# A conv–scan–attention kernel on one core: convolution taps over 128 + 2×64 channels, column sums placed first, in-projection issued between convolution steps

## The chip, the cores and the metric

One core of one Trainium2 chip. The metric is the device time of one execution in microseconds (us). Five engines have instruction queues of their own: TensorE (PE; its weight loads are listed as PEld), VectorE (DVE), ScalarE (ACT), GpSimd (POOL) and SyncE (SP), which issues most DMAs. Each engine takes its instructions in program order and waits on semaphores of the others.

## What is computed

Input `x` is (4, 64, 64, 96). The reference, cut to what matters (per image; `bq` is the sign, `bilinear(x, W) = bq(x) @ (s * bq(W - mean(W))).T + b`):

```python
xz = bilinear(group_norm(x), W_in)            # 96 -> 2*192; only signs of x - mean matter
xp, z = split(xz)
t  = bq(xp + move0_b)                         # signs, 192 channels
t  = conv3x3(t, sc * sign(conv_W))            # 192 -> 192 channels, 9 taps
t  = prelu(t + conv_b + rp_b0) + rp_b1 + xp
u  = silu(t)
for k in 4 directions:                        # rows, columns, and both reversed
    dt, B, C = bilinear(u in direction k, Wl[k])
    delta = softplus(bilinear(dt, Wd[k]) + dt_bias)
    h = exp(delta * A) * h + delta * u * B    # scan over 4096 positions, 192 x 16 states
    y += sum(h * C) + D * u
x = x + bilinear(layernorm(y) * silu(z), W_out)
x = x + linear attention(layernorm(x)) ; x = x + quantized FFN(layernorm(x))
```

## The kernel before

`hybrid_kernel` sets up tiles and calls `run`. The work on each of the NB = 4 images has three parts: a **prologue** (everything up to the scan's operands), the **scans** and an **epilogue** (layer norm, out-projection, attention, FFN).

`Scans.run` is the main loop: 1536 pieces of 128 (32 channels × 4 states) × 1024 positions. A piece is a decay (`dA`, ACT exponential), an injection (`w`, POOL product), a scan (DVE), a product with C (on DVE or POOL, chosen when the program is built by a running tally of both), and a reduction over states (PE, line 1340). The prologue of image b + 1 and the epilogues are generators; one step of them is issued per piece (`next(back)`), so their instructions stand between those of the scans. The prologue of image 0 has nothing to hide behind and runs first, beside the generator `weights()`; `interleave` takes one step of each in turn. In the code this case is `alone = True`; below it is called the head.

The order on every engine is the order of the program text; nothing is rescheduled. What sets it around the change:

- `weights()` issues all loads of weights at its start, on SP: `w_in`, then twelve loads of the convolution's weights (`cw_t`, by input channel, for the products; `cw_n`, by output channel, for their mean size), then the small ones (among them `wrow`, `meanw`, whose rows are gathered in 4-byte elements), ending with `bff`. On ACT it issues `pvd`, twelve loads of `sbR` and 24 loads of `anm` (the A matrix, 32 × 16 elements of 4 bytes each); the signs `wis` of `w_in` come behind these on ACT. Then it signs and transposes the weights (PE, with copies on DVE and POOL) in some 25 steps.
- `prologue`: column sums of x (`csum`, line 514), the negative mean `negm`, eight transposes `xps` whose signs go to `xsT` and whose values go to DRAM through `xb` tiles; the **in-projection**, 16 steps (h, q) for two halves of 96 channels and eight blocks of 512 positions, each with two products (`ix`, `iz`) and two ACT signs: `tp` (the padded image that the convolution reads, in two tiles of 96 channels) and `sz` (the sign of z, stored to DRAM). Then the **convolution**: 16 parts (h, q), each with 18 products of 96×96 weights (9 taps × 2 input halves, line 616) into one PSUM half, then `cz` (line 658), `v` (DVE) and `r` (ACT). In the next part, between the products: two `scalar_tensor_tensor` on DVE, `sg` (signs, copied by three DMAs into `xg`), the exponentials `e`, and `u` on DVE, stored to DRAM in rows (`ud`) and, after a copy on POOL, in columns (`utd`).
- then, for directions (1, 3) and afterwards (0, 2): `xr`, `acc` (the product with Wl), `bcd` and `sgd` to DRAM; `g` is read back, transposed on PE (`gp`, line 761), written to DRAM as `gTd`, and `load_signs` (lines 1161, 1162) reads it into one of two tiles `gT`, from which `prepare` makes delta (line 1202 and on).
- DMAs that go out later are put on a list (`Later`) and issued on SP some steps on. SP is one queue: a DMA is issued after all that stand before it.
- temporary tiles `f32(...)` (xb, sz, v, r, sg, e, u) turn through a pool of 8; the pool `h` has 2.

Of the kernel before, what the change touches and what calls it, by code (L numbers as in the profile page):

```python
# [11 lines left out]
F32 = mybir.dt.float32  # L12
# [13 lines left out]
CH = 1024  # L26
# [19 lines left out]
def halves(src):  # L46

    yield slice(0, 96), 0, src[0:96, 0]
    yield slice(0, 32), 1, src[96:128, 0]
    yield slice(32, 96), 1, src[0:64, 1]  # L50
# [3 lines left out]
def hybrid_kernel(ctx: ExitStack, tc: tile.TileContext, a: dict, out: bass.AP):  # L54
# [14 lines left out]
    def ctile(name, shape, dt=F32):  # L69
        return const.tile(shape, dt, name=name, tag=name)  # L70
# [54 lines left out]
    woutT = ctile("woutT", [96, 2, DM], BF16)  # L125
    cw = ctile("cw", [96, 2, 9, DN], F8)
    csc = ctile("csc", [96, 2])
# [4 lines left out]
    gTs = [ctile(f"gT{i}", [128, 4, 128], F8) for i in range(2)]  # L132
    sbias, cbias = ctile("sbias", [96, 2]), ctile("cbias", [96, 2])

# [23 lines left out]
    def weights():  # L158
# [28 lines left out]
        def transposed(dst, srcs):  # L187

            count[0] += 1
            ps = p.ps.tile([128, 1024], BF16, name=f"tps{count[0]}", tag=f"y{count[0] % 2}")  # L190
            at = 0
            for src in srcs:
                n, f = src.shape
                nc.tensor.transpose(ps[:f, at : at + n], src, identb[:n, :n])
                at += n
            nc.vector.tensor_copy(dst, ps[:f, 0:at], saturate=False if dst.dtype == F8 else None)

        wi = temp("wi", [128, 3, DM], F32)
        nc.sync.dma_start(wi, a["w_in"].rearrange("(t p) j -> p t j", p=128))

        cuts = (slice(0, 5 * DN), slice(5 * DN, 9 * DN))
        cwf, cwn = ([[temp(f"{nm}{h}{i}", [96, s.stop - s.start]) for i, s in enumerate(cuts)] for h in range(2)] for nm in ("cwf", "cwn"))
        for ts, src in ((cwf, a["cw_t"].rearrange("p h t d -> p h (t d)")), (cwn, a["cw_n"])):
            for rows, h, s in halves(src):
                for i, cut in enumerate(cuts):
                    nc.sync.dma_start(ts[h][i][rows], s[:, cut])
        wl = [temp(f"wl{o}", [128, DN], F32) for o in range(2)]
# [31 lines left out]
        nc.gpsimd.memset(bff, 0.0)  # L239
        nc.sync.dma_start(bff[DM : DM + 1, :], a["bff"])  # L240
        nc.scalar.dma_start(pvd, a["pv"][:, :, SD : SD + 3 * NK])
        nc.gpsimd.memset(sbR, 0.0)
# [5 lines left out]
        for g in range(NG):  # L248
            src = a["al"][32 * (g % 4) : 32 * (g % 4) + 32, g // 4].rearrange("d k (q j) -> j d (k q)", j=4)
            for j in range(4):  # L250
                nc.scalar.dma_start(anm[j::4, g, :], src[j])
        for t in gTs + [wdz]:
            nc.gpsimd.memset(t.bitcast(F32), 0.0)

        nc.vector.tensor_tensor(sbias, pv[:, :, B_X], pv[:, :, MOVE0], ALU.add)
        wim = negmean("wim", wi, DM)
        wis = temp("wis", [128, 3, DM], BF16)
        for t in range(3):
            nc.scalar.activation(wis[:, t, :], wi[:, t, :], AF.Sign, bias=wim[:, t : t + 1])
        transposed(winT, [wis[:, t, :] for t in range(3)])  # L260
        yield
        part = temp("part", [96, 2, 2])
        for h in range(2):
            for i, cut in enumerate(cuts):
                nc.scalar.activation(
                    cw[:, h].rearrange("p t d -> p (t d)")[:, cut], cwf[h][i], AF.Sign, saturate=False
                )
                nc.vector.tensor_reduce(part[:, h, i : i + 1], cwn[h][i], AX.X, ALU.add, apply_absolute_value=True)
# [66 lines left out]
        nc.vector.tensor_reduce(dsum, pv[:, :, DSK : DSK + NK], AX.X, ALU.add)  # L335
        nc.scalar.activation(anm, anm, AF.Exp)
        nc.vector.tensor_scalar(anm, anm, -1.0, None, ALU.mult)
        nc.vector.tensor_reduce(sum4, ident.rearrange("p (d j) -> p d j", j=4), AX.X, ALU.add)
# [94 lines left out]
def run(c):  # L433

    made, first = c.weights(), prologue(c, 0, c.xts)
    lanes = [made, first]
    while (0, 1) not in c.ready:
        interleave(lanes)
        c.later.tick()
# [40 lines left out]
def prologue(c, b, xts=None):  # L480
# [11 lines left out]
    with tc.tile_pool(name=f"xg_{b}", bufs=1) as xgp:  # L492
# [3 lines left out]
        with tc.tile_pool(name=f"cv_{b}", bufs=1) as cvp:  # L496
            xsT = cvp.tile([DM, L], F8, name=f"xsT_{b}", tag="xsT")
            tflat = [cvp.tile([96, (IH + 2) * (IW + 2)], F8, name=f"tp{h}_{b}", tag=f"tp{h}") for h in range(2)]
            tpad = [t.rearrange("p (h w) -> p h w", w=IW + 2) for t in tflat]
# [55 lines left out]
            for h in range(2):  # L555
                nc.gpsimd.memset(tflat[h].bitcast(F32), 0.0)
            for h in range(2):
                for q in range(NQ8):
                    cols = slice(512 * q, 512 * q + 512)
                    px, pz = bank(f"ix{h}{q}", 0)[0:96], bank(f"iz{h}{q}", 1)[0:96]  # L560
                    for ps, c0 in ((px, 96 * h), (pz, DN + 96 * h)):
                        nc.tensor.matmul(ps, c.winT[:, c0 : c0 + 96], xsT[:, cols], start=True, stop=True)
                    yield
                    nc.scalar.activation(
                        tpad[h][:, 1 + 8 * q : 9 + 8 * q, 1 : 1 + IW], px.rearrange("p (h w) -> p h w", w=IW),
                        AF.Sign, scale=pv[:, h, S_X : S_X + 1], bias=c.sbias[:, h : h + 1], saturate=False,
                    )
                    sz = f32(f"sz{h}{q}").bitcast(BF16)[0:96, 0:512]
                    nc.scalar.activation(
                        sz, pz, AF.Sign, scale=pv[:, h, S_Z : S_Z + 1], bias=pv[:, h, B_Z : B_Z + 1]  # L570
                    )
                    c.later.store(c.szd[b][h][:, cols], sz)


            yield
            parts = [(h, q) for h in range(2) for q in range(NQ8)]
            taps = [(j, t) for j in range(2) for t in range(9)]
            one = lambda h: slice(h, h + 1)
            prev = turned = None
            two = c.p.dA.tile([128, CH], F32, name=f"cv2_{b}", tag="dA") if alone else None  # L580
            utp = sub.enter_context(tc.tile_pool(name=f"ut_{b}", bufs=1))
# [23 lines left out]
            for n, part in enumerate(parts + [None]):  # L605
                if part:
                    h, q = part
                    nm = f"{h}{q}"
                    at = 512 * (n % 2)
                    ps = (two[:, at : at + 512] if alone else bank("cv" + nm, 0))[0:96]  # L610
                for s in range(4 if alone else 5):
                    if part:
                        per = 5 if alone else 4
                        for j, t in taps[per * s : min(18, per * s + per)]:
                            dy, dx = divmod(t, 3)
                            nc.tensor.matmul(  # L616
                                ps, c.cw[:, j, t, 96 * h : 96 * h + 96],
                                tpad[j][:, 8 * q + dy : 8 * q + dy + 8, dx : dx + IW],
                                start=(j == 0 and t == 0), stop=(j == 1 and t == 8),
                            )  # L620
                    if s == 0 and turned:
                        by_columns(*turned)
                        turned = None
# [46 lines left out]
        with tc.tile_pool(name=f"rw_{b}", bufs=1) as rw:  # L670
# [4 lines left out]
            tbg, sgg = (t.rearrange("p (g r) -> p g r", r=64) for t in (tbc, sgn))  # L675
            g2 = rw.tile([128, 2, 320], F8, name=f"g_{b}", tag="g")
            gw = g2.bitcast(F32)
            for o in (1, 0):
# [74 lines left out]
                if o:  # L753
                    nc.gpsimd.memset(gw[:, :, 48:80], 0.0)
                for x, k in enumerate((o, o + 2)):
                    nc.sync.dma_start(gw[:, x, 0:48], c.sgd[b][k].rearrange("(p f) -> p f", p=128))
                    yield
                    yield
                    gp = bank(f"gp{k}", k // 2).rearrange("p (s f) -> p s f", s=4)
                    for s in range(4):  # L760
                        nc.tensor.matmul(
                            gp[:, s, :], g2[:, x, 48 * s : 48 * s + 128], c.ident8, start=True, stop=True
                        )
                    yield
                    t = rw.tile([48, 4, 32], F32, name=f"gt_{b}_{k}", tag="gt", bufs=2)
                    nc.scalar.activation(t.bitcast(F8), gp[0:48], AF.Copy, saturate=False)
                    nc.sync.dma_start(c.gTd[b][k], t)
# [360 lines left out]
class Scans:  # L1128
# [6 lines left out]
    def __init__(self, c):  # L1135
# [9 lines left out]
        self.late, self.cys = None, {}  # L1145
        self.us, self.gs, self.at, self.loaded, self.sums = {}, {}, -1, set(), {}

# [213 lines left out]
    def run(self, back):  # L1361
# [4 lines left out]
        for x in range(3):  # L1366
# [5 lines left out]
            )  # L1372
        interleave(lanes)
        for q in range(NQ):
            self.load_bc(0, self.bt, 0, 0, 0, q)
            self.load_bc(1, self.ct, 0, 0, 0, q)
# [124 lines left out]
```

## Time and profile before

| | us |
|---|---|
| device time, four runs | 5529.95 to 5538.66, median 5532.41 |
| the profiled execution: device time | 5531.33 |
| the profiled execution: span, first to last instruction | 5529.5 |
| first convolution product in the head | 85.09 |
| last `r` of the convolution in the head starts | 186.45 |
| first `xr` copy | 200.69 |
| first product of `prepare` (line 1202) | 234.78 |
| first scan | 271.19 |

Busy over the span: DVE 91%, POOL 90%, ACT 65%, PE 63%. "Busy" of PE is modelled from pipelined instructions. In the timeline a row has the start, the duration, the engine, the line, the operation, output <- input and how many instructions were merged; in brackets stands the idle time of the engine ahead of it and what ended it. `SPq` and `ACTq` rows are issues of DMAs; their duration is that of the issue, not of the transfer. The windows view gives the busy time of each engine in a stretch, the granted TensorE clock (PEclk, 1.00 is full) and the DMA share.

### The profile page before, as it was taken

To read this page: it belongs to the slowest core of one execution; us is meant where nothing else is said; L and a number is where in the kernel's file an instruction comes from. 1 tells how busy PE (TensorE), PEld (TensorE's weight loads), DVE (VectorE), ACT (ScalarE), POOL (GpSimd) and SP (SyncE) were. 2 spreads that over 40 slices of the span, in tenths; PEclk is the share of its full clock that TensorE was granted. 3 is DMA by queue.
4 is the path that set the end of the run, shared out by engine and by line. 5 is a ranking of instruction groups with operands and counts; after the bars stand their busy time and mean duration, and the time that the engine had idled before them with its cause. 6 is when DMAs were issued, how large, how long until landed. Compare 5 with 4: busy or idle time off the path is not lost. (4 is left out here: it accounts for less than half of the span.)

```text
span 5529.5 us, 62184 instructions
## 1 busy us (share of the span) xinstructions
PE 3489.3 (63%) x20133; PEld 1373.0 (25%) x20133; DVE 5024.9 (91%) x3198; ACT 3568.6 (65%) x5568; POOL 4974.8 (90%) x2255
## 2 busy tenths in 40 slices
PE   5456765467656776657765686664677664445677
PEld 2222222123222222222222232221232221111223
DVE  3299999999999999999999999999999999999984
ACT  4467766677666667777666666776556775555554
POOL 2199999899999999999999999999999999999981
PEclk8666776677766776677776777666787676565787
DMA  4455765766666666676765666667666556666652
GB/s 80 120 187 192 211 199 190 237 223 207 204 192 203 195 201 211 193 239 211 221 191 185 204 205 195 199 207 230 201 214 192 181 191 202 210 201 191 207 157 60
DMA packets 613243, 1069.92 MB, mean 193 GB/s; under 512 B 225083, under 2 KB 343924, under 8 KB 611124
## 3 DMA queue, kind: packets, MB, share of 16 engines
q1 hardware_dynamic: 599428, 1065.88, 61.9%
q8 instruction: 158, 2.59, 0.2%
q10 hardware_dynamic: 13488, 0.07, 0.1%
q14 instruction: 169, 1.38, 0.1%
HBM read 833.20 MB, written 229.38 MB: 192 GB/s over the span
## 5 line engine op out<-in xcount | busy, mean ns | idle before, releaser
L404 POOL TENSOR_TENSOR w<-dl,bc 128x1024 f32<-128x1024 f32 x1536 | 3578.4, 2355 | 159.5 <-PE yp L1340 61.3
L1267 ACT ACTIVATE dA<-dl,anm 128x1024 f32<-128x1024 f32 x1536 | 1714.6, 1116 | 494.2 <-DVE w L404 279.9
L404 DVE TENSOR_TENSOR_SCAN dA<-dA,cy,w 128x1024 f32<-128x1024 f32 x711 | 1665.8, 2343 | 98.7 <-ACT dA L1267 93.6
L1340 PE MATMUL yp<-w,sum 128*32 128x256 f32 x12288 | 1287.7, 514 | 396.1 <-POOL w L404 250.0
L404 POOL TENSOR_TENSOR w<-h,bc 128x1024 f32<-128x1024 f32 x587 | 1380.7, 2352 | 115.8 <-DVE h L404 108.1
L404 DVE TENSOR_TENSOR w<-dA,bc 128x1024 f32<-128x1024 f32 x949 | 1162.3, 1225 | 48.6 <-issue 0.9
L404 DVE TENSOR_TENSOR_SCAN h<-dA,cy,w 128x1024 f32<-128x1024 f32 x441 | 1031.6, 2340 | 10.1 <-ACT dA L1267 10.0
L1340 PEld LDWEIGHTS yp<-w,sum 128*32 128x32 f32 x12288 | 315.2, 129 | 1480.3 <-issue 698.6
L1309 ACT COPY cy<-dA 128x1 f32<-128x1 f32 x715 | 112.2, 157 | 746.0 <-DVE w L404 744.2
L404 DVE TENSOR_TENSOR_SCAN dA<-dA,w 128x1024 f32<-128x1024 f32 x238 | 543.3, 2283 | 29.4 <-ACT dA L1267 20.5
L616 PE MATMUL cv<-tp,cw 96*96 96x512 fp8e5 x1152 | 371.9, 459 | 44.3 <-ACT r L656 40.3
L404 DVE TENSOR_TENSOR_SCAN h<-dA,w 128x1024 f32<-128x1024 f32 x146 | 332.5, 2278 | 10.7 <-ACT dA L1267 9.0
L1202 PE MATMUL dps<-gT,wdz 128*128 128x64 fp8e5 x1000 | 113.6, 313 | 336.3 <-ACT ys L1354 308.0
L1215 PE MATMUL dps<-sp,ident 128*128 128x512 f32 x376 | 282.2, 841 | 50.0 <-ACT dps L1211 49.9
L1345 PE MATMUL yp<-ya,back 128*128 128x256 f32 x576 | 240.4, 539 | 1.8 <-DMA ya<-y 1.0
L616 PEld LDWEIGHTS <-cw 96*96 96x96 fp8e5 x1152 | 156.2, 147 | 238.1 <-issue 188.5
L1202 PEld LDWEIGHTS <-wdz 128*128 128x128 fp8e5 x1024 | 94.8, 152 | 422.9 <-issue 389.5
L1202 PE MATMUL dps<-gT,wdy 128*128 128x64 fp8e5 x504 | 59.9, 323 | 204.1 <-ACT ys L1354 202.0
L1309 ACT COPY cy<-h 128x1 f32<-128x1 f32 x437 | 81.4, 186 | 148.1 <-DVE h L404 146.9
L1207 ACT ACTIVATE pd<-dps,dbias,pvd 128x512 f32<-128x512 f32 x188 | 143.2, 762 | 21.9 <-PE dps L1202 21.6
L1345 PEld LDWEIGHTS yp<-ya,back 128*128 128x128 f32 x576 | 124.5, 250 | 131.1 <-issue 88.6
L878 PE MATMUL yc<-eys,mean 96*96 96x512 f32 x240 | 136.3, 722 | 29.6 <-DVE vks L404 13.7
(290 smaller groups left out, 4223.3 us busy)
## 6 DMA issues: line engine op xcount, KB each, us to landing
dl<-dld SPq DMA_DIRECT2D x768, 512.0 KB
bc<-bcd SPq DMA_DIRECT2D x512, 512.0 KB
dld<-pd SPq DMA_DIRECT2D x125, 512.0 KB
yd<-ys SPq DMA_DIRECT2D x768, 64.0 KB
dld<-pd SPq DMA_DIRECT2D x126, 256.0 KB
ya<-yd SPq DMA_DIRECT2D x192, 128.0 KB
pu<-ud SPq DMA_DIRECT2D x32, 512.0 KB
pu<-utd SPq DMA_DIRECT2D x30, 512.0 KB
```

What stands on the lines that cost most here:

```text
L404: return getattr(self.eng, name)(out, *args, **kw)
L616: nc.tensor.matmul(ps, c.cw[:, j, t, 96 * h : 96 * h + 96], tpad[j][:, 8 * q + dy : 8 * q + dy + 8, dx : dx + IW], start=(j == 0 and t == ...
L878: self.c.nc.tensor.matmul(ps, w, x, start=(i == 0), stop=(i == len(pairs) - 1))
L1202: nc.tensor.matmul(pv[:, s], wd[:, k, s], gT[:, :, c0 : c0 + 16], start=(s == 0), stop=(s == 7))
L1207: nc.scalar.activation(d[:, 0], ps, AF.Abs, scale=sc, bias=bi)
L1215: nc.tensor.matmul(ps, c.ident, t, start=False, stop=True, skip_group_check=True)
L1267: c.nc.scalar.activation(t, self.dlt[i // NQ][0], AF.Exp, scale=c.anm[:, g, NQ * KORD[e] + q : NQ * KORD[e] + q + 1])
L1309: self.c.nc.scalar.copy(self.carries[g, q], h[:, CH - 1 : CH])
L1340: c.nc.tensor.matmul(y[32 * x : 32 * x + 32, g % 2, :], c.sum4, prod[:, 256 * x : 256 * x + 256], start=(q == 0), stop=(q == NQ - 1 and no ...
L1345: c.nc.tensor.matmul(y[:, g % 2, :], w, src, start=False, stop=(n == len(more) - 1))
```

## The change

Parts that go together:

1. The convolution's input channels lie as one tile of 128 channels and one tile that holds the other 64 channels twice, in its lower and its upper 64 partitions, the upper copy moved by one column. One product over the second tile so serves two taps of a line; 9 + 3 × 2 = 15 products a part. The weights lie to match in `cwA` and `cwB` (a quarter of `cwB` is zero). For the second tile the in-projection has weights `winB` (the 64 columns twice) and two ACT signs instead of one. This holds for all four images. Steps per part stay 5 (4 in the head).
2. In the head, the first step of `weights()` and the first six steps of the prologue (column sums to `gsum`) are issued before the two are interleaved.
3. The 24 loads of `anm` are issued on SP, behind `bff`, instead of on ACT; their exponential and negation move from `weights()` to `Scans.run`.
4. In the head, four of the 16 in-projection steps are issued ahead of the convolution, the other twelve between the convolution's steps, two to a part in the first six parts, in the order (q, h). They share one PSUM tile; `sz` lies in the pool `h` (two tiles).
5. For the first direction of the first image the transposed `g` is copied by two ACT copies straight into `gT` (a second set of four PE products puts it at partition 64), with no trip through `gTd`.

```diff
-        cwf, cwn = ([[temp(f"{nm}{h}{i}", [96, s.stop - s.start]) for i, s in enumerate(cuts)] for h in range(2)] for nm in ("cwf", "cwn"))
...
+        for i, cut in enumerate(cuts):
+            nc.sync.dma_start(cfa[i], a["cw_t"][:, 0].rearrange("p t d -> p (t d)")[:, cut])
+        low, high = (a["cw_t"][r0 : r0 + 64, 1].rearrange("p (y x) d -> p y x d", x=3) for r0 in (0, 64))
+        for i, line in enumerate(lines):
+            for x in range(2):
+                nc.sync.dma_start(cfb[i][0:64, :, x], low[:, line, 2 * x])
+            nc.sync.dma_start(cfb[i][64:128, :, 0], high[:, line, 1])
+            nc.gpsimd.memset(cfb[i][64:128, :, 1], 0.0)
...
             for j in range(4):
-                nc.scalar.dma_start(anm[j::4, g, :], src[j])
+                nc.sync.dma_start(anm[j::4, g, :], src[j])
...
     made, first = c.weights(), prologue(c, 0, c.xts)
     lanes = [made, first]
+    next(made)
+    for _ in range(6):
+        next(first)
...
+            two = [c.p.dA.tile([128, CH], F32, name=f"cv{i}_{b}", tag="dA") for i in range(2)] if alone else None
+            def project(h, q):
...
+                nc.tensor.matmul(px, c.winB if h else c.winT[:, 0:128], xsT[:, cols], start=True, stop=True)
...
+                yield
+                for rows, back in ((slice(0, 64), 0), (slice(64, 128), 1)) if h else ((slice(0, 128), 0),):
+                    nc.scalar.activation(
+                        tpad[h][rows, 1 + 8 * q : 9 + 8 * q, 1 - back : 1 - back + IW],
+                        px[rows].rearrange("p (h w) -> p h w", w=IW), AF.Sign,
...
+                sz = c.p.h.tile([128, CH], F32, name=f"sz{h}{q}_{b}", tag="h") if alone else f32(f"sz{h}{q}")
...
+            if alone:
+                ahead = [project(h, q) for q in range(NQ8) for h in range(2)]
+                for g in ahead[:4]:
+                    next(g)
                     yield
+                    next(g, None)
+                del ahead[:4]
...
-            taps = [(j, t) for j in range(2) for t in range(9)]
+            taps = [(tpad[0], c.cwA[:, 3 * dy + dx], dy, dx) for dy in range(3) for dx in range(3)]
+            taps += [(tpad[1], c.cwB[:, dy, x], dy, 2 * x) for dy in range(3) for x in range(2)]
...
-                        per = 5 if alone else 4
-                        for j, t in taps[per * s : min(18, per * s + per)]:
+                        per = 4 if alone else 3
+                        for tp, w, dy, dx in taps[per * s : per * s + per]:
...
+                    if alone and ahead:
+                        if s % 2 == 0:
+                            next(ahead[0])
+                        else:
+                            next(ahead.pop(0), None)
...
+                    gp = columns(k // 2, 64)
+                    if alone and k == KORD[0]:
+                        gp2 = columns(1 - k // 2, 0)
+                        nc.scalar.activation(c.gTs[0][0:48], gp[0:48], AF.Copy, saturate=False)
+                        nc.scalar.activation(
+                            c.gTs[0][64:112, :, 0:112], gp2[64:112, :, 16:128], AF.Copy, saturate=False
                         )
+                        continue
...
         interleave(lanes)
+        c.nc.scalar.activation(c.anm, c.anm, AF.Exp)
+        c.nc.vector.tensor_scalar(c.anm, c.anm, -1.0, None, ALU.mult)
```

## The prediction, made before the changed kernel was run

> **What bounds the kernel now.** I read the page's busy shares first, then busy time by stretch (columns: stretch, its length, busy PE, PEld, DVE, ACT, POOL with instruction counts, granted clock, DMA share, GB/s):
>
> ```profile
> PE 3489.3 (63%) x20133; PEld 1373.0 (25%) x20133; DVE 5024.9 (91%) x3198; ACT 3568.6 (65%) x5568; POOL 4974.8 (90%) x2255
> ```
> ```profile
> 61.00:85.10 24.10, 18.14 (x74) 6.03 (x74) 7.97 (x33) 22.81 (x34) 1.96 (x2) 0.60 0.26 75
> 85.10:187.20 102.10, 77.81 (x305) 40.64 (x303) 46.45 (x62) 48.40 (x78) 15.77 (x15) 0.91 0.30 62
> 271.20:5405.00 5133.80, 3255.62 (x19115) 1255.62 (x19115) 4893.48 (x2963) 3390.95 (x5277) 4915.98 (x2140) 0.70 0.64 202
> ```
>
> From the first scan on, DVE and POOL are each busy over 95% of 5134 us; PE is not the bound there. The head is a serial 271 us: in-projection 61–85 (ACT 22.8 of 24.1), convolution 85–187, directions and delta to 271. So a gain of PE in later images is hidden; a shift in the head counts in full. I then read the head's timeline (start, duration, idle before in brackets).
>
> ```profile
> 31.50 0.90 ACT L259 ACTIVATE slab<-slab,slab 128x96 bf16<-128x96 f32 x3 [29.48 <-DMA anm<-in_al]
> 54.42 0.24 SPq L240 DMA_DIRECT2D bff<-in_bff  x1
> 63.55 22.89 SPq L423 DMA_DIRECT2D szd<-sz  x16
> ...
> 104.08 0.77 ACT L656 ACTIVATE r<-cv,cbias,csc 96x512 f32<-96x512 f32 x1 [1.68 <-DVE v L653]
> 104.91 4.09 PE L616 MATMUL cv<-tp,cw 96*96 96x512 fp8e5 x18 [1.49 <-ACT r L656]
> 105.79 0.59 ACT L597 ACTIVATE sg<-cz 96x512 fp8e5<-96x512 f32 x1 [0.94 <-DVE cz L404]
> 107.56 0.63 ACT L640 ACTIVATE e<-e 96x512 f32<-96x512 f32 x1
> 108.22 0.69 DVE L404 TENSOR_TENSOR u<-cz,e 96x512 f32<-96x512 f32 x1 [2.47 <-ACT e L640]
> 109.03 0.81 DVE L653 TENSOR_SCALAR v<-cv,acs,acb 96x512 f32<-96x512 f32 x1
> 109.87 0.77 ACT L656 ACTIVATE r<-cv,cbias,csc 96x512 f32<-96x512 f32 x1 [1.68 <-DVE v L653]
> ...
> 116.55 5.75 PE L616 MATMUL cv<-tp,cw 96*96 96x512 fp8e5 x18 [1.55 <-ACT r L656]
> ...
> 231.80 0.31 SPq L767 DMA_DIRECT2D gTd<-gt  x1
> 234.78 1.87 PE L1202 MATMUL dA_s<-gT,wdz 128*128 128x64 fp8e5 x16 [3.20 <-DMA gT<-gTd]
> 235.08 5.99 SPq L1233 DMA_DIRECT2D bc<-bcd  x8
> ```
>
> A part of the convolution lasts 5.79 us (r at 104.08 to r at 109.87). Products end at 109.00; u ends at 108.91; v follows both at 109.03. Two chains of equal length close the part: products, and r → cz → sg → e → u, with v behind u in DVE's order.
>
> **The change part by part, against the profiled execution's 5531.33 us** (the median is 1.1 above it).
>
> *Fifteen products, later images.* PE loses 48 products of 0.459 us mean per image, ACT gains 8 signs of about 0.67 us. DVE and POOL keep their instructions and order from the first scan on. DVE's idle beside the three later convolutions (480–800, 1180–1505, 2530–2850) is 18.1 us in all, nearly all ahead of scans that wait for ACT's decay; that is the ceiling of a gain. ACT's 24 signs, 16 us if none were hidden, are the ceiling of a loss. ACT is idle a third of that time: I take −2, with ends −18 and +16.
>
> *Fifteen products, head.* 3 × 0.227 = 0.68 us off the product chain, but u still ends at the same distance from r, so at full clock a part keeps 5.79: nothing is gained. A half-clock stretch of 3.2 us costs 1.6 in a part of 18 (row 116.55: 5.75 us for the products; the part lasts about 7.46); with 15 products the 0.68 of slack is taken off that, so it costs 0.92.
>
> *anm to SP.* On ACT the 24 issues take 0.61 to 1.33 us each (pitch 0.81), 19.5 us, and ACT's first sign stands at 31.50 behind them. That goes: xsT, done at about 60.9, comes near 48.5; the first four projections can start there. But on SP the 24 issues stand behind bff and ahead of the stores of xb and of sz. sz now lies in two tiles, so ACT's third sz waits until the first store of szd has landed. Call that S. The convolution's first product follows it. SP's ledger: loads of w_in and the convolution's weights (2.65 MB, before 10.7 to 31.1) end at 21–26, take 22; they were waiting on two rows of almost 10 us, and less shares the queue. The 23.4 us of small loads (31.24 to 54.66) end at 45. The 24 issues at 0.61–0.81 take 14.6–19.5, take 16: 61. The eight stores of xb (6.8 us before, 54.76 to 61.8) end at 68, and the first szd lands 2–3 us later: **S = 70.5, between 67 and 77**. First product at S + 2 = 72.5 (85.09 before), 12.6 earlier. The exponential and negation of anm in `run` add 0.3 us on ACT, under the bc load.
>
> *Twelve projections beside the convolution.* They were 24 us ahead of it and ACT-bound at 1.46 us a step. Now a part in the first six carries two steps: five signs of 0.67 on ACT (one step with h = 0 has two, one with h = 1 three), and its own 0.77 + 0.59 + 0.58 + 0.63 + 0.63, together 6.55 us, and ACT then waits for the products between (four, and a projection: 1.47). So 8.0 us a part at full clock. PE is idle about 3.5 of 8.0 us, and in the head the granted clock falls to 0.50 after idle stretches of 1.7 us (117.2, 148.0, 161.6, 175.2, each for 3.2 us). At 0.50 throughout a part would be 9.9. I take 9.0. First r ends at S + 12.5: lead 2.0, 15 products at half clock as before (0.427 each, 6.4), 0.81 + 0.77, and 2.5 for the projections' four signs between. Part 1 takes 10.4 with the setup of DVE, four parts at 9.0 and 0.9 for a store that stands behind utd: **r 5 ends at S + 59.8 = 130.3**.
>
> *Ten parts after that.* 57.9 at 5.79. PE's gap per part grows from 1.5–1.7 to 2.2 us as three products go. The falls before come at steps of about 3.4 us, after idle of half such a step or more; a gap of 2.2 covers half a step in 2.2/3.4 of its positions, so about 6.4 of ten parts lose the clock, at 0.92 each: 5.9, ends 2 and 9.2. **r 15 ends at 130.3 + 63.8 = 194.1**; before 186.45 + 0.77 = 187.2. The convolution part as a whole comes out **+6.9**.
>
> One rule bears on the 5.9. The Trainium skill, "TensorE: Matmul & The Clock Gate", section "Part 1: The HAM clock gate", says that the clock falls when PE is idle through a window of about 3.4 us, and stays if no gap is that long. By it gaps of 2.2 us would cost nothing and the sum would be 5.9 lower. The trace shows 0.50 granted after gaps of 1.5 to 1.7 us (row 116.55), so the measurement decides.
>
> *gT without DRAM.* The store (231.80), the reads (232.2) and the wait of 3.20 go; two ACT copies and four products come instead. Line 1202 could start at about 229.3, 5.5 earlier. But the bc loads (235.08 on SP, 4 MB) and the dl load behind them set POOL's start at 261.24; they move from 235.08 to where the u loads end, 231.7. I take **−3.5**, ends −3.4 and −5.5.
>
> Sum: 6.9 − 3.5 − 2 = +1.4 on 5531.33; from the median, **5534**. The measurement tells this kernel from no change at about 0.2%, 11 us: faster is below 5521.3, slower above 5543.5.
>
> **The rivals.**
>
> *Slower: the clock gate takes what the earlier start gave.* One mechanism, in the first six parts and the ten behind. The place: PE between the two projections of a part waits for ACT, its idle share is nearly one half, and a part at 0.50 costs 9.9. If five parts run so (4 × 0.9 = +3.6) and all ten later ones lose the clock (+3.3), r 15 is at 201, the sum is +8.3; with S at 74 in place of 70.5 it is +11.8, at 77 +14.8: 5543 to 5547. It decides from about 4 us more than forecast. For it: half-clock rows in the convolution before with less idle; the granted clock was 0.60 in the stretch where projections ran alone. Against it: 0.91 in the convolution before. The late store of szd belongs to the same side: SP's issues may have the pitch 0.81 in place of 0.64.
>
> *Faster: ACT stays the bound and S is early.* S = 67 (−3.5), parts at 8.0 (4 × 1.0 = −4), ten parts with two of half clock (−3.9), and gT at −5.5 (−2): −13.4 against the forecast, 5520.6. With PE's relief in the later images on top (down to −16 more) 5505. For it: ACT's 8.0 us is a sum of measured rows. Against: all must fall well together; DVE's idle in those stretches is nearly all a wait for ACT, and ACT gets more work.
>
> *It does not do what it says.* The fifteen products save nothing anywhere: u sets the part in the head, DVE and POOL the rest. The forecast has this in it; if also anm on SP delays nothing (S never binds, since sz goes out before), the convolution starts at about 62 rather than 72.5 and the result is −9 or so, near 5523.
>
> **How the numbers follow.** The forecast's own range, from S 67–77, parts 8–9.9, the tail 2–9.2, is about ±10. Forecast and its neighbourhood (inside 0.2%): 0.45. Slower rival and a loss to ACT's signs in later images: 0.31. Faster rival 0.15, and early store or steady relief 0.09: 0.24. Outside the range I leave 0.1 below and 0.1 above: 5517 takes in the faster rival with a part of the steady gain, 5549 the slower with S at 77 and a little of ACT's loss.
>
> **What the changed profile would show.** If right: ACT's third sz has an idle before it that szd's DMA ends, near 70; first product of the convolution 70 to 79; part periods 8 to 10 us for five parts, then 5.8 to 6.7, more rows of fifteen products well over 3.4 us; last r near 194; line 1202 without a wait for gT; DVE and POOL busy within 10 us of 4893 and 4916 in the scans. Wrong: first product below 67 or above 79; periods below 7.5 early on; later parts below 5.7 (then u is not the second chain); a first scan that moves by more than 12 us; or a stretch of scans shorter by more than 10 us, which would show that PE was holding DVE or POOL after all.

## The result, and the profile after

| | before | after |
|---|---|---|
| device time, median | 5533.06 us (53 runs) | 5539.66 us (33 runs) |
| ratio | | 1.0014, 95% interval 1.0009 to 1.0018 |
| span of the profiled execution | 5529.5 us | 5534.2 us |
| first convolution product | 85.09 | 71.81 |
| last `r` of the head's convolution starts | 186.45 | 185.06 |
| first product of `prepare` | 234.78 | 228.61 |
| bc loads start | 235.08 | 231.06 |
| first scan | 271.19 | 268.06 |
| first scan to last scan | 5137.1 | 5145.8 |

The kernel became slower, by 6.6 us in the medians and by 0.14% in the ratio. The time lies in the range and in the case that was held the likeliest, but two terms of the sum were wrong and in part covered each other, which is luck: the head is 3.1 us shorter (3.4 us longer was forecast), and the scans take 8.7 us more (2 us less was forecast).

The head first. These are rows of the changed kernel's timeline, as read before (start, duration, operation, number of instructions, idle time before and what ended it):

```profile
49.53 12.51 SPq L269 DMA_DIRECT2D anm<-in_al  x18
62.16 4.36 SPq L440 DMA_DIRECT2D xbd<-xb  x8
66.61 20.29 SPq L440 DMA_DIRECT2D szd<-sz  x7
69.33 0.77 ACT L600 ACTIVATE sz<-cv,pv 96x512 bf16<-96x512 f32 x1 [12.94 <-DMA szd<-sz]
71.81 1.91 PE L659 MATMUL cv<-tp,cwA 128*96 128x512 fp8e5 x4
...
127.03 2.12 PE L659 MATMUL cv<-tp,cwA 128*96 128x512 fp8e5 x9 [2.94 <-ACT r L703]
...
131.72 0.77 ACT L703 ACTIVATE r<-cv,cbias,csc 96x512 f32<-96x512 f32 x1 [1.52 <-DVE v L700]
132.55 2.12 PE L659 MATMUL cv<-tp,cwA 128*96 128x512 fp8e5 x9 [1.88 <-ACT r L703]
...
135.87 0.69 DVE L421 TENSOR_TENSOR u<-cz,e 96x512 f32<-96x512 f32 x1 [2.52 <-ACT e L687]
136.48 0.80 DVE L700 TENSOR_SCALAR v<-cv,acs,acb 96x512 f32<-96x512 f32 x1
137.31 0.77 ACT L703 ACTIVATE r<-cv,cbias,csc 96x512 f32<-96x512 f32 x1 [1.53 <-DVE v L700]
138.14 3.42 PE L659 MATMUL cv<-tp,cwA 128*96 128x512 fp8e5 x9 [1.96 <-ACT r L703]
...
150.58 2.12 PE L659 MATMUL cv<-tp,cwA 128*96 128x512 fp8e5 x9 [2.01 <-ACT r L703]
...
161.80 3.19 PE L659 MATMUL cv<-tp,cwA 128*96 128x512 fp8e5 x9 [2.00 <-ACT r L703]
...
174.29 2.12 PE L659 MATMUL cv<-tp,cwA 128*96 128x512 fp8e5 x9 [2.06 <-ACT r L703]
...
180.25 2.12 PE L659 MATMUL cv<-tp,cwA 128*96 128x512 fp8e5 x9 [2.32 <-ACT r L703]
```

ACT's third `sz` stood idle for 12.94 us for the store of the first one, which SP could issue only behind anm and the xb stores. A later part lasts 5.59 us (131.72 to 137.31) where 5.79 was measured before. The rows of nine products stand behind PE's gap in each part: after gaps of 1.88, 2.01, 2.06, 2.32 and 2.94 us they take 2.12 us, at full clock; after 1.96 and 2.00 us they take over 3, and the granted clock is 0.50. These two are the only such parts of the ten that hold no projection.

Then the scans. Set side by side scan by scan (the order of DVE's instructions is the same in both kernels), the two executions part in three short stretches, where images 1, 2 and 3 make their in-projection: scans 46 to 66, 262 to 282 and 662 to 682. Windows over exactly these scans (columns as in the prediction: stretch, length, busy PE, PEld, DVE, ACT, POOL, granted clock, DMA share, GB/s), before:

```profile
417.84:486.49 68.65, 45.98 (x234) 13.15 (x230) 63.36 (x38) 56.19 (x91) 65.85 (x31) 0.60 0.60 197
1141.99:1206.54 64.55, 46.56 (x259) 16.02 (x258) 63.02 (x36) 51.80 (x70) 64.55 (x29) 0.74 0.62 203
2479.89:2544.34 64.45, 48.91 (x252) 17.00 (x252) 62.36 (x38) 51.91 (x75) 64.45 (x30) 0.66 0.68 220
```

and after:

```profile
414.79:486.30 71.51, 45.61 (x230) 12.41 (x229) 63.63 (x38) 62.94 (x99) 65.57 (x31) 0.59 0.57 189
1139.56:1207.50 67.94, 49.33 (x256) 16.11 (x256) 63.51 (x36) 58.40 (x78) 65.03 (x29) 0.65 0.60 195
2484.64:2554.96 70.32, 51.19 (x249) 16.60 (x249) 62.86 (x38) 58.49 (x83) 65.91 (x30) 0.62 0.62 200
```

The three lengths add up to 197.7 us before and 209.8 after, +12.1. Each stretch has eight more ACT instructions (91 to 99, 70 to 78, 75 to 83) and 6.6 to 6.8 us more of busy ACT; DVE and POOL have as many instructions as before. In the second and third stretch POOL was busy all the time before, and has idle time after. A piece of the third stretch of the changed kernel shows how:

```profile
2524.31 0.58 ACT L1282 COPY pd<-dps 128x512 f32<-128x512 f32 x1
2524.79 1.56 ACT L593 ACTIVATE tp<-ix,sbx,pvx 64x512 fp8e5<-64x512 f32 x2
2526.37 0.77 ACT L600 ACTIVATE sz<-iz,pv 96x512 bf16<-96x512 f32 x1
2527.05 0.18 ACT L1370 COPY cy<-h 128x1 f32<-128x1 f32 x1
2527.13 1.11 ACT L1328 ACTIVATE dA<-dl,anm 128x1024 f32<-128x1024 f32 x1
2528.34 2.29 DVE L421 TENSOR_TENSOR_SCAN h<-dA,w 128x1024 f32<-128x1024 f32 x1 [0.31 <-ACT dA L1328]
```

Three signs, 2.3 us, stand between the row of `pd` and the decay `dA` of the next scan, which then waits. A sign over 64 partitions takes 0.78 us, as long as one over 128. Outside the three stretches the scans are 3.4 us shorter in this pair of profiles; over all fourteen profiles of this case that remainder scatters from 4930 to 4945 us, so nothing is read from it.

### The profile page after: what moved, and what is told of

Its sections match the earlier page's. It is cut to its first block, busy times and chain, and to the rows that moved or that the text cites. A ratio compares the mean times of both kernels' runs of the same rounds, so it can differ in the third digit from the quotient of the medians.

```text
span 5534.2 us, 61821 instructions
## 1 busy us (share of the span) xinstructions
PE 3436.4 (62%) x19945; PEld 1340.4 (24%) x19945; DVE 5024.2 (91%) x3200; ACT 3594.2 (65%) x5601; POOL 4976.2 (90%) x2261
## 5 line engine op out<-in xcount | busy, mean ns | idle before, releaser
L421 DVE TENSOR_TENSOR_SCAN h<-dA,w 128x1024 f32<-128x1024 f32 x146 | 332.5, 2278 | 12.7 <-ACT dA L1328 11.2
L659 PE MATMUL cv<-tp,cwA 128*96 128x512 fp8e5 x576 | 201.4, 476 | 60.4 <-ACT r L703 57.3
L1406 PEld LDWEIGHTS yp<-ya,back 128*128 128x128 f32 x576 | 122.1, 245 | 130.3 <-issue 90.6
L1269 ACT ACTIVATE sp<-dps,dbias,pvd 128x512 f32<-128x512 f32 x188 | 144.0, 766 | 0.0
```

Of the source, the lines that this page charges most:

```text
L421: return getattr(self.eng, name)(out, *args, **kw)
L659: nc.tensor.matmul(ps, w[:, 96 * h : 96 * h + 96], tp[:, 8 * q + dy : 8 * q + dy + 8, dx : dx + IW], start=(w is taps[0][1]), stop=(w is t ...
L1269: nc.scalar.activation(t, ps, AF.Relu, scale=sc, bias=bi)
L1406: c.nc.tensor.matmul(y[:, g % 2, :], w, src, start=False, stop=(n == len(more) - 1))
```

## The experiments

Times are medians; the kernel before, run beside each group, had 5531.7 to 5533.9 us. The theory after the comparison: the second sign on ACT in the in-projections of images 1 to 3 delays decays, scan after scan. Its rivals: the loss comes from the new order of the head, from the smaller number of products (a lower clock), or is chance. Over all profiles the three stretches leave little to chance: they add up to 197.6 or 197.7 us in the eight kernels without a second sign in images 1 to 3, and to 209.8 or 209.9 us in the five that have the second sign over 64 partitions. The head is less steady: three profiles with the same head (the changed kernel, the copy by DMA, the zero products) have the first scan at 268.1, 265.7 and 269.2 us, and two with the head of the kernel before at 271.2 and 273.8. So a single profile's first scan doesn't tell some 3 us.

**Part 1 alone** (the kernel before with fifteen products; the head's other parts undone).

```diff
-                nc.sync.dma_start(anm[j::4, g, :], src[j])
+                nc.scalar.dma_start(anm[j::4, g, :], src[j])
...
-    next(made)
-    for _ in range(6):
-        next(first)
...
-            if alone:
-
-                ahead = [project(h, q) for q in range(NQ8) for h in range(2)]
-                for g in ahead[:4]:
...
-                    if alone and k == KORD[0]:
+                    if 0:
```

> The kernel before with the fifteen products alone (part 1 of the change, for all images, with the second sign on ACT); everything else as before. Theory A (the second sign on ACT in the in-projections of images 1 to 3 delays the scans' decays): the head's convolution shortens by 0.2 to 0.3 us a part, 3 to 5 us, the later images lose about 8, so +3 to +5 us against the kernel before. Theory B (the loss in the later images comes from the head's other parts, from the order on SP, or from a lower TensorE clock with fewer products): without the other parts the head's gain stays, -3 to -5 us; with the clock as cause, a loss as in A, but sitting in the convolutions rather than in the in-projections.

Measured 5548.38 us against 5532.18, ratio 1.0029 (1.0017 to 1.0040): 16 us slower, worse than both theories said. The three stretches take 71.5, 68.0 and 70.4 us, as in the changed kernel. What had been missed is the head: its in-projection has the second sign too, and there ACT is the bound.

```profile
61.00:94.50 33.50, 21.13 (x110) 8.24 (x110) 11.47 (x36) 32.21 (x48) 5.58 (x20) 0.65 0.25 71
```

ACT is busy 32.2 of 33.5 us; the first convolution product comes at 94.9 instead of 85.1. Of these 9.8 us the sixteen steps account for 5.7 (28.7 us from their first sign, at 66.2, against 23.0 from 62.1): a step with two signs takes 2.26 us, one with a single sign 1.45. The rest is a later start. The convolution itself then makes up for 6 us (first `xr` 204.2 against 200.7), at 5.6 us a part at full clock. The first scan is 5.0 us later than before.

**The sign taken out of images 1 to 3**: the shifted copy is made by two DMAs an image.

```diff
-                for rows, back in ((slice(0, 64), 0), (slice(64, 128), 1)) if h else ((slice(0, 128), 0),):
+                upper = ((slice(64, 128), 1),) if alone else ()
+                for rows, back in (((slice(0, 64), 0),) + upper) if h else ((slice(0, 128), 0),):
...
+                if h and not alone and q % 4 == 3:
+                    n0, n1 = (0, 2177) if q == 3 else (2177, 4355)
+                    c.later.store(tflat[1][64:128, n0:n1], tflat[1][0:64, n0 + 1 : n1 + 1], after=1)
```

> The changed kernel, but in images 1 to 3 the second, shifted copy of the 64 channels is made by two DMAs an image from the lower partitions instead of by eight signs on ACT; the head is untouched. Theory A: the scans get back what the signs cost, 8 us less than the changed kernel (about 5532), and the steps at the in-projections (scans 62 to 63, 271 to 278, 674 to 679) vanish. Theory B: nothing comes back, 5540 as the changed kernel.

Measured 5522.95 us: 16.7 less than the changed kernel's median, 9.2 less than before (ratio 0.9985, 0.9976 to 0.9994). The third stretch:

```profile
2472.91:2537.37 64.46, 48.12 (x249) 16.07 (x249) 62.37 (x38) 51.96 (x75) 64.46 (x30) 0.66 0.68 221
```

It has the length of before again (64.45), and so have the others: 197.7 in all. The 12.1 us are the signs'. That the median fell by more fits a head that happened to be 2.3 us shorter in its profile; the rest is not accounted for and may be scatter.

**The sign put into the kernel before**: the sign of the half h = 1 issued twice in images 1 to 3.

```diff
-                    nc.scalar.activation(
+                    for _ in range(2 if h and not alone else 1):
+                        nc.scalar.activation(
...
```

> The kernel before, with the sign of the in-projection's second half (h = 1) issued twice in images 1 to 3: 24 more signs of ACT, nothing else. Theory A: 8 us slower than before (about 5541), with the delay arising in the in-projections. Theory B: as before, 5533.

Measured 5543.39 us against 5532.18, ratio 1.0020 (1.0011 to 1.0029); the three stretches take 207.9 us, 10.3 more than before. Twenty-four signs, 18.7 us of ACT, cost 10 to 11 us. The theory holds from both sides. What is left of it as delay is 12.1 of 19.9 us of added ACT time in the changed kernel, and about as large a share here.

**The products put back**: as in the DMA version, with three products of zeros a part in images 1 to 3.

```diff
+            if not alone:
+                taps[9:9] = [(tpad[0], None, 1, dx) for dx in range(3)]   # None: a tile of zeros
```

> The kernel e2_copy_by_dma with three more products a part in images 1 to 3, of a tile of zeros (18 products again; the sums are unchanged): is it the smaller number of products that gives anything once the scans run? If DVE and POOL are the bound there, nothing changes: 5523, as e2_copy_by_dma, within its interval. If PE held them, 48 products of 0.46 us an image, up to 66 us in all were saved, and some of it comes back as a loss of over 6 us.

Measured 5522.15 us, against 5522.95 without them. The loss of over 6 us that the rival asked for isn't there. The traces are sharper than the times: scans 66 to 164, beside which nearly all of image 1's convolution is made, take 322.45 to 322.50 us in thirteen of the fourteen profiles (322.84 in the other), with eighteen products a part or with fifteen. The saving for which the layout was changed is hidden there, and only its price shows.

**anm out of the way on SP**: the 24 loads are issued in parts 6 to 11 of the head's convolution.

```diff
-                nc.sync.dma_start(anm[j::4, g, :], src[j])
+                c.anms.append((anm[j::4, g, :], src[j]))
...
+                    if alone and n > 5 and c.anms:
+                        nc.sync.dma_start(*c.anms.pop(0))
```

> The changed kernel, but the 24 loads of anm are issued on SP one to a step in parts 6 to 11 of the head's convolution, behind the stores of xb and sz. If the wait of ACT's third sz for the first store of szd (behind 18.5 us of anm issues on SP) sets the convolution's start: the first store lands near 54 instead of 69, the first product comes near 59 instead of 71.8, and 12 us go from the whole time (about 5527.5). Rival: the transposes of weights on POOL and PE, now hidden in that wait, end next, and only about 5 us go; or the anm issues collide with the stores of ud and utd at the end of the convolution and give half of it back.

Measured 5526.87 us, 12.8 less than the changed kernel.

```profile
51.81 9.40 SPq L441 DMA_DIRECT2D szd<-sz  x4
56.66 0.76 ACT L601 ACTIVATE sz<-cv,pv 96x512 bf16<-96x512 f32 x1
59.13 1.91 PE L660 MATMUL cv<-tp,cwA 128*96 128x512 fp8e5 x4
```

The third `sz` has no idle time before it, the first product comes 12.7 us earlier, and the first scan at 254.1, 14.0 earlier. Neither rival showed.

**Part 5 alone** (the kernel before with g copied straight into gT).

```diff
+                    if alone and k == KORD[0]:
+                        gp2 = columns(1 - k // 2, 0)
+                        nc.scalar.activation(c.gTs[0][0:48], gp[0:48], AF.Copy, saturate=False)
...
-        self.us, self.gs, self.at, self.loaded, self.sums = {}, {}, -1, set(), {}
+        self.gs = {(0, KORD[0]): c.gTs[0]}
+        self.us, self.at, self.loaded, self.sums = {}, -1, set(), {}
```

> The kernel before with part 5 alone: the first direction's transposed g is copied straight into gT. If the bc loads on SP (235.08 before) set the end of the head, only the 3.4 us by which they can move are gained, about 5529; if the first product of line 1202 sets it, 5 to 6 us, about 5527; if the dl load sits behind something else, nothing.

Measured 5532.82 against 5532.84, ratio 0.9996 (0.9988 to 1.0005): inconclusive as a time. In the profile line 1202's work starts 3.6 us earlier, but the bc loads only 1.4 (233.65), and the first scan 1.8, although the convolution ended and the stores of bcd came 1.5 us later there. Counted from the first `xr` all fourteen profiles agree: the bc loads start 34.3 to 35.0 us behind it and the first scan 70.5 to 72.0 in the three without part 5, and 31.4 to 31.7 and 67.0 to 68.8 in the eleven with it. By the middle values part 5 so gives 2.8 us at both. In the kernel before, the changed kernel and this one the dl loads, which POOL waits for, start 19.8, 20.3 and 19.5 us after the bc loads, but 20.1, 22.7 and 21.9 us after the first product of line 1202: they follow the bc loads, not gT. (In all fourteen profiles they start 19.2 to 20.3 us after the bc loads.)

**Part 2 left out** (column sums interleaved again).

```diff
-    next(made)
-    for _ in range(6):
-        next(first)
```

> The changed kernel without part 2: the column sums are interleaved with weights() again. If the wait of ACT's third sz for the store behind anm (until 69.3) sets the start of the convolution, what comes before it has up to 10 us to spare and nothing changes: 5539.7. If the column sums are on the path, 3 to 8 us slower.

Measured 5533.40 us, 6.3 *less* than the changed kernel; the expectation of no effect fell. The third `sz` still waits until 68.6 and the first product stands at 71.4, so the column sums had time to spare. But `weights()` had got further while ACT waited. In the changed kernel the first `v` stands on DVE behind the copy of `woutT`, which waits for a late transpose:

```profile
80.54 0.25 DVE L201 COPY woutT<-tps 96x192 bf16<-96x192 bf16 x1 [2.38 <-PE tps L199]
80.71 0.80 DVE L700 TENSOR_SCALAR v<-cv,acs,acb 96x512 f32<-96x512 f32 x1
```

Without part 2 that copy is done at 70.9, and the first `v` waits for the products alone:

```profile
77.48 0.81 DVE L697 TENSOR_SCALAR v<-cv,acs,acb 96x512 f32<-96x512 f32 x1 [2.78 <-PE cv L656]
```

The first `r` comes at 79.0 instead of 81.55, and the first scan at 263.1, 4.9 us earlier and 2.6 us ahead of the earliest of the three profiles with part 2 and the same head. What the first `r` doesn't explain of it is not shown.

**Part 4 left out** (all sixteen steps ahead).

```diff
-                sz = c.p.h.tile([128, CH], F32, name=f"sz{h}{q}_{b}", tag="h") if alone else f32(f"sz{h}{q}")
+                sz = f32(f"sz{h}{q}")
...
-                ahead = [project(h, q) for q in range(NQ8) for h in range(2)]
-                for g in ahead[:4]:
...
+            ahead = []
+            if 1:
                 for h in range(2):
                     for q in range(NQ8):
                         yield from project(h, q)
```

> The changed kernel without part 4: all sixteen in-projection steps ahead of the convolution, two PSUM banks in turn, sz in the pool of 8 that the xb tiles use too. The order on SP is as in the changed kernel, so the first sz waits for the first store of xb, behind anm, until about 64. Theory of the queue: then sixteen steps of 1.5 to 2.2 us, 30 us, first product at 94 to 96, parts of 5.6 to 6: last r near 190, some 5 us later than in the changed kernel, 5545. Rival (ACT alone counts, and the twelve steps beside the convolution lengthened six parts by 3 us each): last r earlier by 2 to 3, about 5537.

Measured 5541.02 us against 5539.66, which tells neither theory; the profile decides. The theory of the queue holds:

```profile
61.87 4.47 SPq L440 DMA_DIRECT2D xbd<-xb  x8
64.34 0.78 ACT L598 ACTIVATE sz<-iz,pv 96x512 bf16<-96x512 f32 x1 [13.70 <-DMA xbd<-xb]
```

The first product is at 93.7 and the last `r` at 189.7, where the three profiles of the head with part 4 have it at 184.5 to 186.0. The first `xr` comes at 204.0 (199.4 in the changed kernel), the first scan 3.7 us later than there. The order beside the convolution is worth some 4 to 5 us at the last `r`.

**Towards a better version: both repairs together** (the edits of the copy by DMA and of the late anm, unchanged).

> e2_copy_by_dma and e5_anm_late together: the shifted copies of images 1 to 3 by DMA, and the loads of anm late. They act in different stretches, so the gains should add: 5522.95 - 12.8 = 5510. If the later images only gave back what a late start of the scans had cost, or the other way round, 5516 or more.

Measured 5515.39 us. The first scan (253.0) is 12.8 earlier than with the copy by DMA alone, as it should be; of the 12.8 us the medians show 7.6. The scans took 5141 us in this profile and 5133 in the other, with the same scan instructions. Six profiles of kernels with these scans range from 5129 to 5143 us, so one profile doesn't tell 5 us; that an earlier start is partly given back was not settled. Against it stands that the last kernel below has the earliest first scan of all, 239.8, and the shortest scans, 5129 us.

**z out of the first six parts** (product and sign of z, one step a part in parts 6 to 15, six behind the convolution).

```diff
+            late = [project_z(h, q) for q in range(NQ8) for h in range(2)] if alone else []
...
+                    elif alone and late and part and s == 2:
+                        next(late[0])
+                    elif alone and late and part and s == 3:
+                        next(late.pop(0), None)
```

> e7_both, but in the head the half of the in-projection that makes z (product and sign, needed only by the epilogue) is taken out of the first six parts: ten of the sixteen come one to a part in parts 6 to 15, at the step where ACT waits for DVE, the last six behind the convolution, where ACT waits for the columns of u. If ACT bounds the first six parts, as the prediction's 8.0 us a part said, two signs of 0.77 leave each of them, and three or four leave the steps ahead of the convolution: 9 + 3 us less than e7_both, about 5498. If the chain of DVE and PE sets these parts, or the later parts take it back, less than 4 us.

Measured 5506.41 us, 9 less. Four of the first parts last 6.7 us instead of 8.2 to 8.9 (the first of all 8.1): ACT did bound them. But the first scan comes only 2.8 us earlier (250.2 against 253.0), so most of the 9 us of the medians, of five runs each, is not shown to come from this. z found a new wait in the two tiles of its pool (one part of 8.3 us, 8.7 us behind the convolution), which the next step takes away.

**z in eight tiles.**

```diff
-                sign_z(h, q, pz, c.p.h.tile([128, CH], F32, name=f"sz{h}{q}_{b}", tag="h"))
+                sign_z(h, q, pz, c.p.w.tile([128, CH], F32, name=f"sz{h}{q}_{b}", tag="w"))
```

> e8_z_late with the z signs in eight tiles (a pool that is free in the head) instead of two. In e8_z_late the third z of the convolution's end waited for a store of szd that stood on SP behind the 6 us of utd: one part of 8.3 us instead of 5.6, and ACT idle 8.7 us behind the convolution, so that the first xr came 20.1 us after the last r instead of 14.3. If that wait is all, 2.7 + 5.7 us go: about 5498. If utd's own transfer sets the first xr, only 2.7 go, about 5504.

The first scan comes at 241.2, 9.0 earlier, and the first `xr` 14.3 us after the last `r` again: that wait was all. The time, 5505.21 us of five runs, doesn't show it (its profile has the longest scans of the six). Both steps together bring the first scan 11.8 us forward, and the medians fall by 10.2.

**And without part 2** (the edit that leaves it out, made to the version with eight tiles).

> e9_z_buffers without part 2 (column sums interleaved with weights() again). Leaving part 2 out of the changed kernel gained 6 us there, where the store behind anm set the start of the convolution. If the gain came from the steps of weights() that now lie ahead of the convolution and no longer between its first products (first part 8.1 us in e9_z_buffers against 6.7 for the next ones), 1 to 3 us are gained here too, first scan near 239.5 instead of 241.2. If the column sums are on the path once the wait for the store is gone (first product at 55.6 in e9_z_buffers), the first product comes 2 to 4 us later and the first scan at 243 to 245. Either moves the time by less than its interval; the first scan of the profile decides.

First product at 56.2, 0.5 later, but the first `r` 0.7 earlier and the first scan at 239.8, 1.4 earlier. That is as the first reading says, but smaller than the scatter of the head, so it doesn't decide; the 2 to 4 us of loss that the second reading asked for are not there. Measured 5497.41 us against 5533.93, ratio 0.9937 (0.9923 to 0.9951). By the medians this version is 36.5 us faster than the kernel before and 42.3 us faster than the changed one.

## Why the prediction was right or wrong

- *The later images, −2.* Wrong, and the step that failed can be named: ACT's 24 signs were priced at nothing for the likeliest case because "ACT is idle a third of that time". That is about right for the scans as a whole (busy 66%) and for the three windows beside the later convolutions that the prediction names (busy 683 of 965 us, 71%). But the in-projections, where the signs stand, lie for the most part ahead of these windows. There ACT was busy 80 to 82% (51.9 of 64.5 us in the third stretch), the sign stands ahead of the next scan's decay in ACT's program order, and in two of the three stretches POOL had no idle time; so 12.1 of 19.9 us of added ACT time became delay. The bound that was kept (16) held it; the value inside it was taken from the wrong window. The other half of the step was right: fewer products bring nothing there, shown with the zero products.
- *anm on SP, S.* Right: the third `sz` waited for the store behind anm, until 69.3 (forecast 70.5, within 67 to 77), first product 71.8 (72.5). Two errors of the ledger nearly cancelled: the issues of anm took 17.8 us (16 taken), the stores of xb 4.4 (6.8 taken). Moving the loads away brought the first product 12.7 us forward.
- *The first six parts.* Right: bound by ACT, as taking z out showed, 8.2 to 9.5 us (9.0 taken). `r` 5 ended at 127.0 where S + 59.8 made 130.3; 0.7 of this is the earlier start, and the rest is spread over the first `r`, the setup of DVE and a wait for a store.
- *The ten parts behind, 63.8.* Wrong: 58.9 (126.98 to 185.83). The period at full clock was 5.6, not 5.79. The two chains of the prediction were not of equal length: from `r` to u it is 4.14 us before and 4.15 after, but v, which no longer waits for the products, starts 0.61 us behind u instead of 0.81. And only two of the ten parts lost the clock, not 6.4, though all gaps were 1.5 to 2.9 us; each cost 1.2 us, not 0.92. The prediction put the gaps before at 1.5 to 1.7 us, and the limit at half a step of 3.4; the row that it names has 1.55. In all profiles the granted clock changes at whole multiples of 3.41 us from one another. Counting PE's idle time in each such step of the convolution that ran at full clock, the clock fell behind steps with 1.55 us and more in the kernel before and stayed behind those with up to 1.49; in the changed kernel's late parts it fell behind 1.96, 2.00 and 2.68 and stayed behind up to 1.91. So here a gap of 2 us counted only where it lay almost wholly within one step, which few did; why the limit lies higher with fifteen products is not shown. The Trainium skill, "TensorE: Matmul & The Clock Gate", section "Part 1: The HAM clock gate", has the clock fall after an idle window of about 3.4 us. The two parts of 6.8 us after gaps of 1.96 and 2.00 us contradict it, though 57.9, the sum without any loss, was nearer to 58.9 than the 63.8. So the convolution's end moved by −1.4 instead of +6.9.
- *gT, −3.5.* Right in its mechanism (the bc loads bind), somewhat too large in size: over all profiles 2.8 us at the bc loads and at the first scan. In the pair of before and after, the bc loads start 4.0 us earlier and the first scan 3.1, which is 2.6 and 1.7 more than the last `r` gained.
- *Rivals.* Neither mechanism of the slower rival (late S, half clock throughout) came; the loss had another place. Of the faster one only the few losses of the clock in the late parts came. That fifteen products save nothing was right for images 1 to 3; in the head they took 6 us off the convolution, which the first kernel of the experiments lost again to the second sign and a later start.
- *Column sums first.* The prediction has no term for part 2. It kept `weights()` back, which cost 2.5 us at the first `r` of the pair (1.3 to 2.5 against the three profiles with the same head).

## What to carry to other kernels

An engine's idle share over a long stretch says little about the cost of an added instruction: read its busy time in the window where the instruction will stand, and whose next instruction it is queued ahead of. A DMA moved to another queue is paid by whatever stands behind it and by the buffers that wait for that; load late what is needed late, and give what waits for a store more buffers. When the engine that is relieved is not the bound, ask where the price is paid, and pay it with a DMA if those have time.

## What the runs showed of the hardware

A sign on ACT over 64 partitions took 0.78 us, as one over 128 did, for 512 elements each: splitting by partitions doubles the cost. Gaps of 1.96 and 2.00 us between products were followed by half clock for about 3.4 us, those of 2.01, 2.06, 2.32 and 2.94 us were not: the length of a gap alone doesn't decide. What fits these traces is PE's idle time (by the modelled ends of the products) within one step of 3.41 us: the clock fell from 1.55 us on in the kernel before, and from 1.96 us on in the changed kernel. Seven more profiles with fifteen products fit a limit of 1.95 us; one, with products of z between the late parts, has a fall behind 1.71. The 24 loads of `anm` (32 × 16 elements of 4 bytes each) held SP's queue for 17.8 us, 0.74 each.
